# Products of softmax weights with values, taken for two key tiles together at every other step of the first attention

## The chip, the cores and the metric

The kernel runs on one core of a Trainium2 chip. The metric is the device time of one execution in microseconds (us). Before the change the median of three runs is 1603.94 us (1602.0 to 1604.71).

## The reference, cut to what matters

The whole program is a small transformer block for 1024 tokens of width 512: a first attention, a mixture-of-experts layer, a second attention with 4-bit weights, and the same mixture-of-experts layer again, each on a layer norm of the running sum `x`. The change touches only the first attention:

```python
q = hidden_state @ wq + bq          # 32 heads of 16
k = hidden_state @ wk + bk          # 8 groups of 16, each shared by 4 heads
v = hidden_state @ wv + bv
scores = jnp.einsum('bhqd,bhkd->bhqk', q, k) * scale
probs = jax.nn.softmax(scores, axis=-1)
out = jnp.einsum('bhqk,bhkd->bhqd', probs, v)
out = jnp.swapaxes(out, -1, -2).reshape(B, -1, HEAD_DIM * NUM_HEADS)
return out @ wo + bo
```

## The kernel before, in words

**Tiles.** The first attention goes through 16 pairs of heads (`PAIRS`), and for each pair through 8 tiles of 128 keys (`NT`). One (pair, key tile) is called a step here, so there are 128 steps, and a step is written (pair, kt).

**What a step computes.** Scores are computed twice. First with queries on the partitions, only to find each query's largest score: `half_score` (L333) is one matmul of 64 rows (L340) into a PSUM bank `sc` and one VectorE maximum over its 512 columns (L349). There are 512 of these, 4 in each step, and they run 40 ahead of the rest (`LEAD`), so that those of one pair are done during step 5 of the pair before it. When a pair's 32 are done, three small VectorE instructions (L352 to L354) join the halves and split the result into two parts in `largest`; `place_largest` (L359) turns that on TensorE (L363), copies it on ScalarE (L365) and lets SyncE's queue carry it to the rows of `ms_q` (L367).

Then the scores are computed again with keys on the partitions: `exponentials` (L376) takes for each of four parts `u` (two heads, two halves of the queries) one matmul (L381), one more that adds the negated maxima (L389), and the exponential on ScalarE (L393) into `pT`. `weighted` (L407) multiplies `pT` with the values: four matmuls (L414), whose outputs of 32 partitions lie side by side in one bank `po` and which run at once in four strips of 32 columns of the array. The trace holds two records for each, so a `weighted` shows as 8 records. After the last key tile, `po` is copied to `oT` (L423), which `tail` (L428) turns back (L434) and divides by the sums (L438, L439).

**Buffers.** There are 8 PSUM banks: three for `sc`, four for `st` (which `mp`, `pt`, `py` and `pp` share), one for `po`. `pT` has three buffers.

**Order.** On TensorE the order is the one written (L495, `manual_schedule`). On the other engines the tile framework lays the order down when the kernel is built, and it executes as laid down. `side_by_side` (L399) interleaves two chains: one on rows 0 to 63 of the array (three scores, the two matmuls of part 2, the fourth score), one on rows 64 to 127 (the two matmuls of parts 0, 1 and 3). A step therefore begins with six rounds, each of two matmuls that run at once in the two halves of the rows. The fourth score is in round six, and the rounds below are numbered so. After the rounds comes, at even key tiles, `place_largest` where maxima are ready, and then `weighted` of the step before (`behind`, L519). At `kt == 3` the tail of the pair before follows, at `kt` 5 and 7 of pairs 4, 8 and 12 a part of the output projection (`project_out`, L448), at `kt` 1 and 3 of pairs 3 and 7 the queries of later heads (`queries`, L287), and at `kt == 7` the loads of keys and queries for three pairs later (L298).

The scores are used up at step (14,5): 40 + 4 x 118 = 512. The last ten steps have none.

Of the kernel before, what the change touches and what calls it, by code (L numbers as in the profile page):

```python
# [41 lines left out]
def kernel(  # L42
# [159 lines left out]
    def attention_a():  # L202
# [6 lines left out]
        with ExitStack() as ph:  # L209
# [77 lines left out]
            def queries(c, half, *between):  # L287
                if half == 0:
                    q_hls[c] = work.tile([P, 2, S], F32R, tag="q_hl", name="q_hl")
                split(q_hls[c], ts(half, C), lambda k: wq_n[:, c, k], bq_sb[:, c : c + 1], *between)  # L290

            def stack_keys(g, eng):
                for r in range(8):
                    eng.dma_start(
                        ks[g % NS][ts(r, DA)].bitcast(F32), k_hl[ts(g, DA), r % 4 // 2].bitcast(F32)
                    )
# [16 lines left out]
            def values(t):  # L313
                pv = st_ps.tile([P, C], F32, tag="st", name="pv")
                for c in range(NC_):
                    nc.tensor.matmul(
                        pv[:, : G * DA],
                        xT[:, c, ts(t, P)],
                        wv_n[:, c, :],
                        start=(c == 0),  # L320
                        stop=(c == NC_ - 1),
                    )
                nc.vector.tensor_tensor(
                    v_sb[:, t, :, :DA],
                    pv[:, : G * DA].rearrange("p (g d) -> p g d", d=DA),
                    bv_b.rearrange("p (g d) -> p g d", d=DA),
                    ALU.add,
                )
# [30 lines left out]
            def place_largest():  # L359
                for pair in list(large):  # L360
                    both = large.pop(pair)
                    mp = st_ps.tile([P, C], F32, tag="st", name="mp")
                    nc.tensor.transpose(mp[:, :P], both.bitcast(F32), ident)  # L363
                    mT = work.tile([32, P], F32R, tag="mT", name="mT")
                    nc.scalar.copy(mT, mp[:32, :P])  # L365
                    for r in (0, 64):
                        nc.sync.dma_start(  # L367
                            ms_q[pair % 2][r : r + 2]
                            .bitcast(F32)
                            .rearrange("h j (t q) -> h (j t) q", q=P),  # L370
                            mT.bitcast(F32),
                        )
# [3 lines left out]
            def exponentials(pair, kt, u, rows):  # L376

                if u == 0:
                    pTs[pair, kt] = work.tile([P, 4, C], F32, tag="pT", name="pT", bufs=3)
                st = st_ps.tile([P, C], F32, tag="st", name="st")  # L380
                nc.tensor.matmul(  # L381
                    st,
                    ks[pair // 2 % NS][rows, ts(kt, P)],
                    qs[pair % NS][rows, u // 2, ts(u % 2, C)],
                    start=True,
                    stop=False,
                )
                yield
                nc.tensor.matmul(  # L389
                    st, ones[rows], ms_q[pair % 2][rows, u // 2, ts(u % 2, C)], start=False, stop=True  # L390
                )
                yield
                nc.scalar.activation(pTs[pair, kt][:, u], st, AF.Exp, scale=DA**-0.5)  # L393

            def chain(*parts):
                for part in parts:
                    yield from part

            def side_by_side(*two):  # L399

                two = list(two)
                while two:
                    for one in list(two):
                        if next(one, two) is two:
                            two.remove(one)

            def weighted(pair, kt):  # L407


                if kt == 0:  # L410
                    pos[pair] = av_ps.tile([P, C], F32, tag="po", name="po")
                po, pT = pos[pair], pTs.pop((pair, kt))
                for u in range(4):
                    nc.tensor.matmul(  # L414
                        po[ts(u, 32), :],
                        v_sb[:, kt, pair // 2, :],
                        pT[:, u],
                        start=(kt == 0),
                        stop=(kt == NT - 1),
                    )  # L420
                if kt == NT - 1:
                    oT = work.tile([P, C], F32, tag="oT", name="oT", bufs=1)
                    nc.vector.tensor_copy(oT, pos.pop(pair))  # L423
                    tails.append((pair, oT))
# [23 lines left out]
            def project_out(a, h):  # L448

                py = st_ps.tile([P, C], F32, tag="st", name="py")
                for c in range(NC_):
                    nc.tensor.matmul(  # L454
                        py,
                        o_sbs[a][:, 4 * h + c, :],
                        wo_n[:, c, :],
                        start=(c == 0),
                        stop=(c == NC_ - 1),
                    )  # L460
                nc.vector.tensor_tensor(x_sb[:, a, h, :], x_sb[:, a, h, :], py, ALU.add)
# [16 lines left out]

            LEAD = 40
            n_score = 0
            low, high = slice(0, 64), slice(64, 128)

            def next_score(rows):
                nonlocal n_score
                n_score += 1
                if n_score <= 32 * PAIRS:
                    yield from half_score(n_score - 1, rows)

            def scores(n):
                for _ in range(n // 2):
                    side_by_side(next_score(low), next_score(high))

            with tc.manual_schedule(engines={mybir.EngineType.PE}):  # L495
                for t in range(NT):
                    values(t)
                scores(4)
                for half in range(2):
                    queries(1, half, lambda: scores(2))  # L500
                scores(16)
                place_largest()
                scores(LEAD - n_score)
                behind = None
                for pair in range(PAIRS):
                    for kt in range(NT):
                        side_by_side(
                            chain(
                                next_score(low),
                                next_score(low),  # L510
                                next_score(low),
                                exponentials(pair, kt, 2, low),
                                next_score(low),
                            ),
                            chain(*[exponentials(pair, kt, u, high) for u in (0, 1, 3)]),
                        )
                        if kt % 2 == 0:
                            place_largest()
                        if behind is not None:  # L519
                            weighted(*behind)  # L520
                        behind = pair, kt
                        if kt == 3:
                            for item in tails:
                                tail(*item)
                            tails.clear()
                        if kt in (5, 7) and pair % 4 == 0 and pair:
                            project_out(pair // 4 - 1, (kt - 5) // 2)
                        if kt == 7 and pair + NS < PAIRS:
                            if (pair + NS) % 2 == 0:
                                stack_keys((pair + NS) // 2, nc.sync)  # L530
                            stack_queries(pair + NS)
                        if kt in (1, 3) and pair in (3, 7):
                            queries(pair // 4 + 2, kt // 2)
                weighted(*behind)

                for a in range(3):
                    norm.stats(a)
                norm.scale(0, 3)
                for item in tails:
                    tail(*item)  # L540
                for a in range(3):
                    xn = wq_in[:, 2 * (a % 2) : 2 * (a % 2) + 2]
                    norm.rows(a, xn)
                    norm.turned(
                        a, xn, lambda: st_ps.tile([P, C], F32, tag="st", name="tp"), False, to_xT
                    )
                    if a:
                        project_out(3, a - 1)
# [610 lines left out]
```

## Time and profile before

| | us |
|---|---|
| median of three runs | 1603.94 |
| the profiled execution, its own time | 1603.51 |
| its span, from first to last instruction | 1601.4 |
| steps with scores, 82 to 466 us of the span | 384 |
| steps without scores, 466 to 492 us | 26 |
| all after the first attention's steps, 492 us to the end | 1109 |

Busy time of the engines in these three stretches:

| stretch | TensorE | VectorE | ScalarE | granted clock |
|---|---|---|---|---|
| 82 to 466 us | 377.24 | 324.41 | 250.89 | 1.00 |
| 466 to 492 us | 25.97 | 1.60 | 19.53 | 1.00 |
| 492 to 1601 us | 1069.27 | 867.53 | 497.33 | 0.99 |

In the profile PE is TensorE's matmuls, PEld its weight loads, DVE is VectorE, ACT ScalarE, and SPq the queue of DMA issues on SyncE. A row of the timeline gives start, duration, engine, line, operation, output and inputs, and after x the number of instructions merged in it; behind it, in brackets, stands how long the engine was idle before and what released it. The duration of a merged row runs from the start of its first to the end of its last instruction. A busy TensorE is not TensorE at its peak, since matmuls are pipelined and their records overlap.

### The profile page before, as it was taken

The numbers are of one execution on the slowest core, as the hardware profiler recorded it, in microseconds if no ns is written. First come the engines' busy times: TensorE is split into PE (matmuls) and PEld (weight loads), VectorE is DVE, ScalarE is ACT, GpSimd is POOL, SyncE is SP. The second block draws the span as 40 slices with busy tenths as digits, with TensorE's granted clock in tenths as the row PEclk, the third lists the DMA queues.
The fourth block names the chain that finished last, engine by engine and source line by source line (L and its number), as shares of the span: only waits on it lengthen the run. The fifth ranks groups of instructions, "written<-read, shape, count | busy, mean of one in ns | idle before, by whom it ended". The sixth has DMA issues, their size and how long they took to land.

```text
span 1601.4 us, 24101 instructions
## 1 busy us (share of the span) xinstructions
PE 1535.4 (96%) x8119; PEld 994.2 (62%) x8119; DVE 1239.7 (77%) x2290; ACT 784.3 (49%) x1696; POOL 480.8 (30%) x380
## 2 busy tenths in 40 slices
PE   6899999999999989999999999999999999999978
PEld 3444444444445457777777777777777777777764
DVE  3798787799754586788888878888788788788763
ACT  2076565567674235544444544444444444454420
POOL 7000000000103144435436336336336335333120
PEclk9799999999999989999999999999999999999999
DMA  7523223223103233343343334333333333333311
GB/s 237 99 44 66 39 47 54 50 50 58 22 3 91 72 114 115 111 140 122 112 144 127 118 127 130 119 121 124 122 124 117 115 116 125 109 111 124 138 53 53
DMA packets 98010, 158.63 MB, mean 99 GB/s; under 512 B 14320, under 2 KB 53936, under 8 KB 97504
## 3 DMA queue, kind: packets, MB, share of 16 engines
q1 hardware_dynamic: 97024, 155.46, 32.5%
q0 software_dynamic: 864, 1.64, 0.7%
q8 instruction: 65, 1.06, 0.3%
q14 instruction: 57, 0.47, 0.1%
HBM read 33.03 MB, written 6.05 MB: 24 GB/s over the span
## 4 chain that ended last, share of the span: by engine, by line
PE 80%; DVE 11%; ACT 4%; issue 2%; DMA 1%; SPq 1%; POOL 1%; ACTq 0%; DVEq 0%; POOLq 0%
PE pc L877 16%; PE sc L835 14%; PE sc L340 6%; PE po L414 6%; PE pp L771 5%; DVE m L349 5%; PE pp L772 5%; PE tp L867 5%; PE py L771 4%; PE py L772 3%; PE bank L580 3%; PE pp L275 3%; PE st L381 2%; PE py L454 2%; PE st L389 1%
## 5 line engine op out<-in xcount | busy, mean ns | idle before, releaser
L349 DVE TENSOR_REDUCE m<-sc 128x1 f32<-128x512 f32 x512 | 320.0, 681 | 39.4 <-PE st L381 31.0
L844 ACT ACTIVATE x_sb<-sc,m 128x768 f32<-128x768 f32 (+7 forms) x256 | 189.9, 742 | 315.6 <-DVE m L840 310.0
L393 ACT ACTIVATE pT<-st 128x512 f32<-128x512 f32 x512 | 264.9, 603 | 126.6 <-PE st L389 102.5
L835 PE MATMUL sc<-kT,qT 128*128 128x512 f32 (+3 forms) x768 | 292.0, 489 | 3.8 <-ACT x_sb L844 2.4
L840 DVE TENSOR_REDUCE m<-sc 128x1 f32<-128x768 f32 (+7 forms) x256 | 192.6, 752 | 131.0 <-PE sc L838 129.7
L877 PE MATMUL pc<-xT,v_sb 128*128 128x256 f32 (+1 forms) x1024 | 247.8, 373 | 5.2 <-DVE acc L785 2.5
L340 PE MATMUL sc<-ks,qs 64*128 64x512 f32 x512 | 192.6, 464 | 9.8 <-DVE m L349 4.5
L846 DVE TENSOR_SCALAR x_sb<-x_sb,total 128x768 f32<-128x768 f32 (+7 forms) x256 | 189.0, 739 | 4.4
L877 PEld LDWEIGHTS pc<-xT,v_sb 128*128 128x128 f32 x1024 | 175.4, 189 | 22.0 <-DVE acc L785 3.2
L835 PEld LDWEIGHTS sc<-kT,qT 128*128 128x128 f32 x768 | 139.0, 192 | 74.8 <-issue 64.1
L340 PEld LDWEIGHTS sc<-ks,qs 64*128 64x128 f32 x512 | 86.7, 189 | 153.6 <-DVE m L349 130.6
L381 PE MATMUL st<-qs,ks 64*128 64x512 f32 x512 | 178.2, 426 | 1.6 <-ACT pT L393 0.2
L912 DVE SCALAR_TENSOR_TENSOR shared<-py,o_sc,shared 128x512 f32<-128x512 f32 x248 | 176.1, 739 | 4.0 <-PE py L772 3.9
L389 PE MATMUL st<-ms_q,ones 64*128 64x512 f32 x512 | 179.1, 414 | 0.0
L797 POOL TENSOR_TENSOR qT<-acc,cos_sb 128x512 f32<-128x512 f32 x62 | 81.9, 1320 | 301.3 <-DVE total L845 205.3
L771 PE MATMUL pp<-x_hl,w 128*128 128x512 f32 x384 | 167.0, 435 | 1.9 <-DVE acc L785 1.3
L868 ACT COPY xT<-tp 128x512 f32<-128x512 f32 (+2 forms) x320 | 137.4, 471 | 63.2 <-PE tp L867 62.9
L772 PE MATMUL pp<-x_hl,w 128*128 128x512 f32 x384 | 152.9, 398 | 2.3 <-DVE x_hl L729 2.3
L679 POOL TENSOR_SCALAR w<-r 128x512 fp32r<-128x512 int32 x80 | 122.6, 1532 | 105.5 <-PE pp L772 71.2
L785 DVE SCALAR_TENSOR_TENSOR acc<-pp,q_sc,acc 128x512 f32<-128x512 f32 x192 | 142.9, 745 | 13.5 <-ACT acc L783 5.8
L867 PEld LDWEIGHTS tp<-ident_r,moved 128*128 128x128 f32 x1152 | 125.3, 140 | 35.7 <-issue 2.0
L561 POOL TENSOR_TENSOR x_sb<-x_sb,shared 128x1024 f32<-128x1024 f32 x4 | 9.4, 2366 | 449.7 <-ACT wq_in L175 391.5
(167 smaller groups left out, 2303.3 us busy)
## 6 DMA issues: line engine op xcount, KB each, us to landing
turned<-acc SPq DMA_DIRECT2D x160, 128.0 KB
qs<-q_hl SPq DMA_DIRECT2D x256, 64.0 KB
moved<-x_sb SPq DMA_DIRECT2D x32, 512.0 KB
moved<-x_sb SPq DMA_DIRECT2D x32, 448.0 KB
moved<-x_sb SPq DMA_DIRECT2D x32, 384.0 KB
moved<-x_sb SPq DMA_DIRECT2D x32, 320.0 KB
r<-in_qwq_dram SPq DMA_DIRECT2D x32, 256.0 KB
r<-in_qwo_dram SPq DMA_DIRECT2D x32, 256.0 KB
```

The lines of the kernel that those rows point to most:

```text
L340: nc.tensor.matmul(sc, qs[pair % NS][rows, jj, ts(t, P)], ks[pair // 2 % NS][rows, ts(half, C)], start=True, stop=True,)
L349: nc.vector.tensor_reduce(ms[pair][:, at : at + 1], sc, AX.X, ALU.max, negate=True)
L381: nc.tensor.matmul(st, ks[pair // 2 % NS][rows, ts(kt, P)], qs[pair % NS][rows, u // 2, ts(u % 2, C)], start=True, stop=False,)
L389: nc.tensor.matmul(st, ones[rows], ms_q[pair % 2][rows, u // 2, ts(u % 2, C)], start=False, stop=True)
L393: nc.scalar.activation(pTs[pair, kt][:, u], st, AF.Exp, scale=DA**-0.5)
L771: nc.tensor.matmul(ps, lhsT, high, start=True, stop=False)
L772: nc.tensor.matmul(ps, lhsT, low, start=False, stop=True)
L835: nc.tensor.matmul(sc[:, k0:k1], qT[:, ts(t, P)], kT[:, k0:k1], start=True, stop=(k1 < keys))
L840: nc.vector.tensor_reduce(m, sc[:, :keys], AX.X, ALU.max, negate=True)
L844: nc.scalar.activation(p[:, :keys], sc[:, :keys], AF.Exp, bias=m, accum_out=total)
L867: nc.tensor.transpose(tp[:, k - k0, :].bitcast(F32R), p[:, ts(k, P)], ident_r)
L877: nc.tensor.matmul(pc[:, 2 * P * i + lo : 2 * P * (i + 1)], v_sb[:, k, ts(g, DB)], place[pair][:, k, lo:], start=(k == 0), stop=(k == 2 * ...
```

## The change

`behind` becomes a list. At an even key tile every step in it is taken through `weighted`, and the list is emptied; at an odd key tile nothing is multiplied with the values. So after an even step there come the products of two key tiles, 16 records in a row where there were 8. In step (p,0) these are tiles 6 and 7 of the pair before; in steps (p,2), (p,4), (p,6) they are tiles 0 and 1, 2 and 3, 4 and 5. The last two come after the loop.

```diff
-                behind = None
+                behind = []
                 for pair in range(PAIRS):
                     for kt in range(NT):
...
                         if kt % 2 == 0:
                             place_largest()
-                        if behind is not None:
-                            weighted(*behind)
-                        behind = pair, kt
+                        if kt % 2 == 0:
+                            for item in behind:
+                                weighted(*item)
+                            behind.clear()
+                        behind.append((pair, kt))
...
-                weighted(*behind)
+                for item in behind:
+                    weighted(*item)
```

In the built program, the numbers of instructions are the same on every engine. On VectorE the order changes as well: before, L352 to L354 stand after the fourth maximum of step (p,5), one behind the other. After, for all pairs but 4, 8, 12 and 14, they stand after the first, second and third maximum of step (p,6), one behind each. In pairs 5, 9 and 13 some statistics of the layer norm move by a few places. On ScalarE one row of the layer norm and four exponentials trade places, on SyncE's queue four of the loads of keys and queries do. Beyond the first attention no engine's order changes.

## Prediction

> **What bounds the kernel now.** I first read the 40 slices and the groups of the page: in the stage that changes, TensorE is busy everywhere and VectorE nearly so, so that neither share tells which of them sets the pace. I then asked for the waits between 82 and 493 us.
>
> ```profile
> engine line waited for: us in total, times, longest us
> ...
> PEld sc L340 <- DVE m L349: 115.7, 199, 1.2
> ...
> DVE m L349 <- PE st L381: 31.0, 72, 3.9
> ```
>
> The score's weight load waits for a maximum, because there are three `sc` banks. The maximum in turn waits for TensorE in most steps. They take turns, so the timeline of a step decides. Two plain steps on TensorE, and the same stretch on VectorE:
>
> ```profile
> 284.26 1.06 PE L414 MATMUL po<-pT,v_sb 128*32 128x512 f32 x8
> 285.25 0.49 PE L340 MATMUL sc<-ks,qs 64*128 64x512 f32 x1
> ...
> 285.59 0.39 PE L340 MATMUL sc<-ks,qs 64*128 64x512 f32 x1
> ...
> 285.82 0.39 PE L340 MATMUL sc<-ks,qs 64*128 64x512 f32 x1
> ...
> 286.53 0.50 PE L340 MATMUL sc<-ks,qs 64*128 64x512 f32 x1
> ...
> 286.97 1.06 PE L414 MATMUL po<-pT,v_sb 128*32 128x512 f32 x8
> ```
>
> ```profile
> 285.79 2.48 DVE L349 TENSOR_REDUCE m<-sc 128x1 f32<-128x512 f32 x4 [0.48 <-PE st L381]
> 288.50 2.48 DVE L349 TENSOR_REDUCE m<-sc 128x1 f32<-128x512 f32 x4 [0.22 <-PE st L381]
> 290.90 0.68 DVE L423 COPY oT<-po 128x512 f32<-128x512 f32 x1
> ```
>
> A plain step takes 286.97 - 284.26 = 2.71 us: 0.99 from the burst of L414 to the first round, then 1.72 of rounds. Four maxima take 2.48, each 0.68 long and (2.48 - 0.68) / 3 = 0.60 apart, so 4 x 0.60 = 2.40 of steady work. VectorE is idle only 0.22 a step: it lives through the burst on maxima in stock. The fourth score starts at 286.53, just as the first maximum is done (285.79 + 0.69 = 286.48). Both engines are at their limit.
>
> **The change part by part.** No instruction goes or comes. There are half as many bursts, each twice as long, and twelve rounds in a row.
>
> *The burst.* The second half of the records of L414 starts 0.45 after the first, and fp32 matmuls in a row (records of L275 at 263.12, 263.55, 263.98) start 0.43 apart. A double burst is thus 0.99 + 2 x 0.43 = 1.86, and at most 1.98.
>
> *A plain pair of steps, worked out.* Time 0 is the first round after a burst. From the rows above: rounds at 0, 0.33, 0.57, then each 0.23; the first maximum starts at 0.54, then one each 0.60; a bank is free 0.05 after its maximum; after a round that waited, the next comes 0.33 later; the burst follows an unwaited last round by 0.32 (301.50 to 301.83).
> - Maxima start at 0.54, 1.14, 1.74, 2.34, 2.94, 3.54, 4.14, 4.74; each ends 0.68 later, the first at 1.23, the last at 5.42.
> - Scores 1 to 3 at 0, 0.33, 0.57; 4 (round 6) at 1.28; 5 needs the second maximum's bank: 1.87; 6 the third's: 2.47; 7 the fourth's: 3.07; 8 (round 12) at 3.07 + 0.33 + 0.23 + 0.23 = 3.86, its bank being free at 3.67.
> - Burst from 3.86 + 0.32 = 4.18 to 6.04.
>
> So 6.04 in place of 2 x 2.71 = 5.42: **+0.62**. At the burst's start VectorE has 5.42 - 4.18 = 1.24 of work in stock, and the next maximum comes 1.86 + 0.54 = 2.40 later: it idles 1.16 where it idled 2 x 0.22.
>
> *The price of the array's change of form, weighed.* Around a burst the trace shows 0.54 from its second half to the next round (0.43 within a row), 0.33 to the second round (0.23), 0.32 at the entry (0.23): 0.30 for each burst. The Trainium skill, TensorEngine Tiling (Array Packing), Key Properties, says that changing the tiling mode, not just the tile, drains the array. By this rule alone, one change fewer in each of the 59 pairs of steps with scores (to step (14,5)) would give 59 x 0.30 = 18 us of gain. By the rows the gain lies within TensorE's time, which the working above already has, while the maxima set the end. The rule's saving is real, but goes into waiting.
>
> *The four kinds of pairs of steps.* Before, from the starts of L414:
> - Steps 1 and 2, 2.98 + 2.71 = 5.69. The copy of `po` stands before the next maximum. Now VectorE is idle when the burst ends, so it costs only 0.20 (maximum at 0.74 in place of 0.54): 6.24, +0.55.
> - Steps 3 and 4, 3.75 (298.08 to 301.83) + 2.71 = 6.46. The tail now lies between the rows. Its transposes run from 1.71 to 2.29, the fifth score goes at 2.29, later ones at 2.63, 3.07. The tail's four small VectorE steps (0.6 to 0.8 together, between maxima) delay maxima 5 to 8 to 3.06, 3.98, 4.73, 5.33. One `st` bank is held by the tail, so part 3 waits for the exponential of part 0, to 3.80 (as at 301.17 before), and the burst goes at 4.46: 6.32, -0.14.
> - Steps 5 and 6, 2.71 + 3.28 = 5.99. L352 to L354 now stand after maxima 5, 6 and 7. VectorE takes its queue in order, so L354 comes behind three more maxima: 2.94 + 0.60 (L352 at 3.54), maximum at 3.66, L353 at 4.27, maximum at 4.39, L354 at 5.0 to 5.18. The transpose L363 stands on TensorE before the burst and waits for that: 5.24 where the rounds would let it go at 4.3. Then 0.26 to the burst as before, and 1.86: 7.36, **+1.37**. Behind L363 queue the burst and every later score.
> - Steps 7 and 0: plain, 6.04, +0.62.
>
> *Count.* Plain kinds: 9 of the first at 0.55 and pair 0 (three steps before the first burst) at 0.5; 11 of the second at -0.14, pair 0 without a tail at +0.62; 11 of the third at 1.37, pair 14 at +0.25; 11 of the fourth at 0.62. That is 5.5 - 0.9 + 15.3 + 6.8 = 26.7. In ten pairs of steps a block of 3.6 us (`queries`, `project_out`) lies between the rows; VectorE catches up in it, and one entry and exit is saved: 10 x -0.17 = -1.7. In pairs 5, 9, 13 layer-norm steps of VectorE fall into its new idle time: -1.2. Without scores, ScalarE's exponentials (0.48 apart, 8 in a pair of steps, four `st` banks) hold the rows by 0.2 in four pairs of steps: +0.8. Sum **+24.6 us**, before to after, in one profiled execution of 1603.51 us (its span of 1601.4 and 2.1 around it); that execution lies 0.4 us under the median, so I put the median at 1603.94 + 24.6 = 1628.5.
>
> *What I cost at nothing.* `pT`: with three buffers an exponential of an odd step needs the buffer that the first half of the burst reads; the next exponential starts some 0.86 after the rows begin, and both halves are over by then. Without that cover it would be 0.43 a pair of steps. `po`: its next use now comes two steps after the copy. `ms_q`: L363 to first use was 4.3 us (252.93 to 257.23) and is 4.6. The moved loads on SyncE's queue have a pair of heads (24 us) to land, and the transfer share is 0.26 here; nothing waits for them before beyond 0.3 us. After the loop the chain on TensorE goes on as before, so 492 us and later are only shifted.
>
> *Bounds.* No row shows maxima with a double burst. Best for VectorE: all three banks full at the burst's start, 1.80 in stock: it still idles 0.60, and a plain pair takes 4.88 + 0.60 = 5.48, no gain. So the plain kinds can't go below zero by more than the trace's grain; with the mixed pairs at -3 and the second kind at -1.5 the lower bound is about -5 us. Upper: if the tail and the norm steps hide nothing, 12 x 0.76 + 1.2 = 10 us more. The wait at L363 is the largest single unknown: 0 to 0.94 us, 11 times. I take its full value, as VectorE's order is laid down and its pace of 0.60 is the nearest row.
>
> **The rivals.**
> 1. *TensorE sets the end, and the saved changes of form are gained.* Price -0.30 a burst, 59 times: 1604 - 18 = 1586, faster. For it: TensorE is the busiest engine, with 80% of the chain. It decides from the point where VectorE's stock at the burst reaches 2.40 us, four maxima; three banks hold 1.80. Against it stands the 0.22 of idle after each single burst.
> 2. *L363 doesn't wait*, because L354 comes earlier than worked out: 11 x 0.75 less, 1628.5 - 8 = 1620. For it: before, L363 never waited for L354 (only 3.8 us for ScalarE, 15 times). Against it: the order of the built program.
> 3. *The tail hides nothing*: steps 3 and 4 lose as plain ones do, 11 x 0.76 more, 1637.
> 4. *No change*: the starved maxima are made good by the mixed pairs and the emptier chain, 1604.
>
> **How the numbers follow.** My working 0.66, rival 2 0.18, rival 3 0.09, rival 4 0.03, rival 1 0.04. The predicted time is the first's, 1628.5. The range reaches over rival 2, with 4 us for its own errors, and to rival 3: 1616 to 1637. About 0.2% is what a measurement of this kernel can tell from no change. Faster 0.04, same 0.03, slower 0.93.
>
> **What would show it.** In the changed profile a plain pair of steps takes about 6.0 us between bursts; the burst of L414 shows 16 records in 1.9 us; VectorE's idle time before L349 grows from 32.6 us in this stage to 70 or more (59 x 0.72 more at the most), with L381 or L340 as releaser; L363 waits for L354 by 0.9 in pairs without a projection; in steps 3 and 4 the period is about 6.3. The stage from 82 to 492 us is longer by 24, the rest is not. I am wrong if the plain pair stays at 5.4 or less (rival 1 or 4), if L354 ends before the twelfth round (rival 2), or if the stages after the first attention move.

## The result, and the profile after

The changed kernel takes 1626.16 us, the median of four runs (1625.74 to 1627.03), where the kernel before, measured alongside, takes 1602.97 (1598.57 to 1604.71). The ratio is 1.0149 (95% interval 1.0131 to 1.0166). The medians differ by 23.2 us and the ratio makes it 24, where 24.6 was worked out. The profiled execution has a span of 1623.6 us, 22.2 more than before.

The same plain pair of steps that the prediction worked out, here steps (5,7) and (6,0) on TensorE and then on VectorE:

```profile
235.88 1.93 PE L414 MATMUL po<-pT,v_sb 128*32 128x512 f32 x16
237.73 0.50 PE L340 MATMUL sc<-ks,qs 64*128 64x512 f32 x1
...
238.07 0.39 PE L340 MATMUL sc<-ks,qs 64*128 64x512 f32 x1
...
238.30 0.39 PE L340 MATMUL sc<-ks,qs 64*128 64x512 f32 x1
...
239.01 0.49 PE L340 MATMUL sc<-ks,qs 64*128 64x512 f32 x1
...
239.61 0.50 PE L340 MATMUL sc<-ks,qs 64*128 64x512 f32 x1
...
240.21 0.50 PE L340 MATMUL sc<-ks,qs 64*128 64x512 f32 x1
...
240.80 0.50 PE L340 MATMUL sc<-ks,qs 64*128 64x512 f32 x1
...
241.61 0.39 PE L340 MATMUL sc<-ks,qs 64*128 64x512 f32 x1
...
241.93 0.64 PE L414 MATMUL po<-pT,v_sb 128*32 128x512 f32 x4
```

```profile
238.26 4.88 DVE L349 TENSOR_REDUCE m<-sc 128x1 f32<-128x512 f32 x8 [2.17 <-PE sc L340]
243.92 0.69 DVE L423 COPY oT<-po 128x512 f32<-128x512 f32 x1 [0.78 <-PE po L414]
```

The burst is one row of 16 records, 1.85 us to the next round. The first three scores come at once; then scores 4 to 7 come 0.60 apart, the pace of the maxima, because each waits for its bank, as the weight load of the fifth shows:

```profile
239.61 0.18 PEld L340 LDWEIGHTS sc<-ks,qs 64*128 64x128 f32 x1 [0.41 <-DVE m L349]
```

The eight maxima run without a gap for 4.88 us, end at 243.14, and the next score is not there before the burst from 241.93 is over: VectorE stands idle. From burst to burst 241.93 - 235.88 = 6.05 us, 5.42 before.

The pair of steps with L352 to L354, (5,5) and (5,6), on VectorE and at its end on TensorE:

```profile
230.97 3.08 DVE L349 TENSOR_REDUCE m<-sc 128x1 f32<-128x512 f32 x5 [0.90 <-PE st L381]
233.97 0.16 DVE L352 TENSOR_TENSOR m<-m 128x16 f32<-128x16 f32 x1
234.06 0.68 DVE L349 TENSOR_REDUCE m<-sc 128x1 f32<-128x512 f32 x1
234.66 0.16 DVE L353 CAST largest<-m 128x16 fp32r<-128x16 f32 x1
234.73 0.68 DVE L349 TENSOR_REDUCE m<-sc 128x1 f32<-128x512 f32 x1
235.33 0.17 DVE L354 TENSOR_TENSOR largest<-m,largest 128x16 fp32r<-128x16 f32 x1
235.41 0.68 DVE L349 TENSOR_REDUCE m<-sc 128x1 f32<-128x512 f32 x1
```

```profile
235.64 0.30 PE L363 MATMUL mp<-ident,largest 128*128 128x128 f32 x1 [0.94 <-DVE largest L354]
```

L354 stands behind three maxima and ends at 235.50; L363 has waited 0.94 us for it, and the burst behind L363 with it. In the kernel before, the same three stood together at the start of that stretch, and L363 had no wait:

```profile
227.68 0.18 DVE L352 TENSOR_TENSOR m<-m 128x16 f32<-128x16 f32 x1
227.89 0.17 DVE L353 CAST largest<-m 128x16 fp32r<-128x16 f32 x1
228.10 0.17 DVE L354 TENSOR_TENSOR largest<-m,largest 128x16 fp32r<-128x16 f32 x1
```

```profile
229.36 0.33 PE L363 MATMUL mp<-ident,largest 128*128 128x128 f32 x1
```

The periods of pairs of steps, from the starts of the bursts in the two traces (in "mixed" pairs of steps queries or a part of the projection lie between the rows, in "plain" ones not):

| steps | plain, before | plain, after | worked out | mixed, after less before |
|---|---|---|---|---|
| 1 and 2 | 5.70 | 6.26 | 6.24 | -0.22 |
| 3 and 4 | 6.45 | 6.32 | 6.32 | -0.13 |
| 5 and 6 | 5.99 | 7.28 | 7.36 | -0.14 |
| 7 and 0 | 5.41 | 6.05 | 6.04 | -0.16 |

All 62 pairs of steps between the bursts of steps (0,2) and (15,6) take 402.7 us before and 426.7 after, 24.0 more. With the ends of the loop, from the first L381 to the start of the last burst, it is 24.5 more (413.2 and 437.7). The span grew by less, 22.2: the loop started 3.5 us earlier in the execution after (first L381 at 73.5 us, before at 77.0), where the two programs are the same, and from the last burst on the two need 1111.1 and 1112.4 us. The prediction put both at nothing. The early start fits the granted clock, whose mean up to the first L381 is 0.89 after (8.1 us short of full clock) and 0.85 before (11.6 us short), but no run tested it.

The wait list of the changed stage, 82 to 516 us:

```profile
PEld sc L340 <- DVE m L349: 102.1, 220, 0.8
...
DVE m L349 <- PE st L381: 41.2, 36, 2.9
...
DVE m L349 <- PE sc L340: 25.0, 12, 2.2
...
PE mp L363 <- DVE largest L354: 10.3, 11, 0.9
```

From the list of the kernel before, besides the two lines that the prediction shows:

```profile
DVE m L349 <- PE sc L340: 1.4, 4, 0.5
```

Before its maxima VectorE waits in fewer places (36 and 12, before 72 and 4) and for longer: 66.2 us in all, before 32.4. The last line of the changed kernel's list is new: eleven waits, 0.9 each.

### The profile page after: what moved, and what is told of

Its sections match the earlier page's. It is cut to its first block, busy times and chain, and to the rows that moved or that the text cites. A ratio compares the mean times of both kernels' runs of the same rounds, so it can differ in the third digit from the quotient of the medians.

```text
span 1623.6 us, 24111 instructions
## 1 busy us (share of the span) xinstructions
PE 1543.5 (95%) x8119; PEld 1002.9 (62%) x8119; DVE 1234.1 (76%) x2290; ACT 789.6 (49%) x1696; POOL 480.2 (30%) x380
## 3 DMA queue, kind: packets, MB, share of 16 engines
HBM read 33.03 MB, written 6.05 MB: 24 GB/s over the span
## 4 chain that ended last, share of the span: by engine, by line
PE 55%; DVE 4%; ACT 2%; issue 1%; DMA 0%; POOL 0%; ACTq 0%; DVEq 0%; SPq 0%
PE pc L881 16%; PE sc L839 15%; PE pp L775 5%; PE pp L776 5%; PE tp L871 4%; PE py L775 3%; PE py L776 3%; PE bank L584 1%; DVE m L844 1%; PE sc L842 1%; PE bank L572 1%; DVE acc L789 1%; ACT x_sb L848 1%; ACT xT L872 0%; PE bank L645 0%
## 5 line engine op out<-in xcount | busy, mean ns | idle before, releaser
L349 DVE TENSOR_REDUCE m<-sc 128x1 f32<-128x512 f32 x512 | 318.6, 680 | 71.7 <-PE st L381 41.2
L393 ACT ACTIVATE pT<-st 128x512 f32<-128x512 f32 x512 | 268.9, 604 | 148.1 <-PE st L389 138.6
L340 PE MATMUL sc<-ks,qs 64*128 64x512 f32 x512 | 208.2, 469 | 15.3 <-DMA qs<-q_hl 2.9
L839 PEld LDWEIGHTS sc<-kT,qT 128*128 128x128 f32 x768 | 139.5, 192 | 74.7 <-issue 63.9
L381 PE MATMUL st<-qs,ks 64*128 64x512 f32 x512 | 184.9, 435 | 0.6 <-ACT pT L393 0.2
```

What stands on the lines that cost most here:

```text
L340: nc.tensor.matmul(sc, qs[pair % NS][rows, jj, ts(t, P)], ks[pair // 2 % NS][rows, ts(half, C)], start=True, stop=True,)
L349: nc.vector.tensor_reduce(ms[pair][:, at : at + 1], sc, AX.X, ALU.max, negate=True)
L381: nc.tensor.matmul(st, ks[pair // 2 % NS][rows, ts(kt, P)], qs[pair % NS][rows, u // 2, ts(u % 2, C)], start=True, stop=False,)
L839: nc.tensor.matmul(sc[:, k0:k1], qT[:, ts(t, P)], kT[:, k0:k1], start=True, stop=(k1 < keys))
```

## The experiments

Theory S is the prediction's: the three score banks hold too little work for VectorE to live through a double burst. Rival T: the long burst or the twelve rounds are slow on TensorE itself. Rival A: the exponentials on ScalarE set the pair of steps. All periods below are those of plain pairs of heads, from the starts of the bursts of L414 (L417 where lines are added ahead of it).

**VectorE and ScalarE taken out of the way.** Two kernels, from the one before and the changed one:

```diff
-                nc.vector.tensor_reduce(ms[pair][:, at : at + 1], sc, AX.X, ALU.max, negate=True)
+                nc.vector.tensor_reduce(ms[pair][:, at : at + 1], sc[:, : C // 4], AX.X, ALU.max, negate=True)
...
-                    pTs[pair, kt] = work.tile([P, 4, C], F32, tag="pT", name="pT", bufs=3)
+                    pTs[pair, kt] = pT_all[(NT * pair + kt) % 3]
...
-                nc.scalar.activation(pTs[pair, kt][:, u], st, AF.Exp, scale=DA**-0.5)
+                nc.scalar.activation(pTs[pair, kt][:, u, : C // 4], st[:, : C // 4], AF.Exp, scale=DA**-0.5)
```

`pT_all` (its lines are left out) are three tiles that are made once and filled with 1.0 ahead of the loop.

Expected of the first:

> The kernel before, with each maximum taken over the first 128 of its 512 columns and each exponential over the first 128 of its 512 queries (the rest of the weights stay at 1.0): VectorE and ScalarE should no longer hold anything, so TensorE alone sets a step. All theories: a plain step 2.57 us (0.99 + 0.33 + 4 x 0.23 + 0.32), where the kernel before has 2.71. It is the base for the next run.

Expected of the second:

> The changed kernel with the same two cuts. Theory S (VectorE starves in the double burst, because three score banks hold too little): with VectorE out of the way only the saved change of the array's form is left: 0.33 + 10 x 0.233 + 0.32 + 1.86 = 4.84 for a plain pair of steps against 5.14, so -0.30, and some 19 us less than the base over 64 pairs of steps. Rival T (the double burst or the twelve rounds in a row are slow on TensorE itself): a pair stays at 5.4 or more, and the kernel is no faster than the base.

Measured: 1574.01 us (1572.12 to 1579.79) with single bursts and 1563.63 (1561.02 to 1565.89) with double ones. Against the kernel before the ratios are 0.9825 (0.9796 to 0.9854) and 0.9759 (0.9733 to 0.9786), so the double bursts now **gain** some 10 us, half of the 19 that I expected. A plain pair takes 5.16 and 5.02, and in the steps without scores 5.15 to 5.19 and 4.83. So rival T falls: TensorE itself is faster with double bursts. The saving of 0.30 a pair, which the prediction read from the rows, shows whole (0.32 to 0.36) only where there are no scores. With scores it is 0.14, because one wait for a bank is left. The sixth and seventh score of a plain pair with double bursts:

```profile
212.31 0.39 PE L340 MATMUL sc<-ks,qs 64*128 64x512 f32 x1
...
212.62 0.18 PEld L340 LDWEIGHTS sc<-ks,qs 64*128 64x128 f32 x1 [0.33 <-DVE m L349]
212.62 0.50 PE L340 MATMUL sc<-ks,qs 64*128 64x512 f32 x1
```

The seventh score starts 0.31 after the sixth, not 0.23, and takes 0.50; its weight load, which waited for a maximum, starts with it and not ahead of it. The round after it comes 0.34 later. It needs the bank of the fourth score, three rounds before: even a maximum of 0.29 us is not done in three rounds of 0.23.

**Only the maxima shortened** (the first hunk alone):

> The kernel before with only the maxima cut to 128 of 512 columns. Theory S: VectorE idle, ScalarE keeps up with single bursts: a plain step 2.58 to 2.60, as in the ten steps without scores.

> The changed kernel with only the maxima cut. Theory S: the starved maxima were the bound, and next is ScalarE through its four banks, as in the steps without scores (5.46 a pair there): a plain pair 5.2 to 5.5, so 0.55 to 0.85 less than 6.05. Rival A (ScalarE's exponentials were the bound all along, the maxima only wait with them): a plain pair stays at 6.0.

Measured, one execution each: 1584.57 and 1591.40 us. Steps 7 and 0 took 5.53 to 5.66 with single bursts, above what I expected (5.16 to 5.20, which steps 1 and 2 did take), and 5.49 with double ones, as expected. With single bursts the first use of `ms_q` in step (p,0) now waits for its transfer, 0.36 in the mean, about what is missing:

```profile
PEld st L389 <- DMA ms_q<-mT: 4.3, 12, 0.4
```

Rival A falls, since 6.05 became 5.49 by VectorE alone. But with short maxima the double bursts gain nothing either. They cost about 0.3 in steps 1 and 2 and in steps 5 and 6: now 108 weight loads of L381 wait for an exponential's bank (28 with single bursts, 16.8 us).

```profile
PEld st L381 <- ACT pT L393: 31.8, 108, 1.6
```

So there are two stocks, three banks for VectorE and four for ScalarE, and the longer burst outlasts both.

**The number of score banks**, two, three and four, in the changed kernel. For two only `sc` is changed, from 3 to 2. For four, `st` must give one up, so ScalarE is taken out of the way by the exponential's cut above, and a base with three is run the same way:

```diff
-            sc_ps = pool(ph, "a_sc_ps", 3, PSUM)
-            st_ps = pool(ph, "a_st_ps", 4, PSUM)
+            sc_ps = pool(ph, "a_sc_ps", 4, PSUM)
+            st_ps = pool(ph, "a_st_ps", 3, PSUM)
```

> The changed kernel with two score banks in place of three. Theory S: VectorE has one maximum less in stock when the burst begins, so a plain pair of steps grows by about 0.6, to 6.65 to 6.75 us (worked out: score 8 at 4.43, burst from 4.86 to 6.72). Rivals T and A: the number of score banks doesn't matter, 6.05.

> The changed kernel with three score banks and three st banks, each exponential over the first 128 of its 512 queries (the rest of the weights stay at 1.0), so that ScalarE holds nothing. Base for the next run. Theory S: unchanged, a plain pair of steps 6.05 us, because the maxima set it. Rival A (the exponentials set it): well under 6, towards 5.2.

> The same with four score banks and three st banks. Theory S: one maximum more in stock, 0.60 less idle: a plain pair of steps 5.44 to 5.5. Rivals T and A: as the run with three score banks.

| score banks | whole kernel, one execution | steps 7 and 0 | expected | VectorE idle before the copy of `po` that follows |
|---|---|---|---|---|
| two | 1687.28 | 6.83 | 6.65 to 6.75 | 1.19 |
| three (exponentials cut) | 1640.43 | 6.05 | 6.05 | 0.79 |
| four (exponentials cut) | 1637.47 | 5.46 | 5.44 to 5.5 | 0.19 |

Burst to burst with four banks:

```profile
240.00 1.92 PE L417 MATMUL po<-pT,v_sb 128*32 128x512 f32 x16
...
243.12 0.66 PE L340 MATMUL sc<-ks,qs 64*128 64x512 f32 x2
...
245.12 0.40 PE L340 MATMUL sc<-ks,qs 64*128 64x512 f32 x1
...
245.45 1.49 PE L417 MATMUL po<-pT,v_sb 128*32 128x512 f32 x11
```

A fourth and fifth score now stand one behind the other with no wait between. The fourth bank is one maximum, 0.60 us, in stock, and moves the pair by 0.59. With the exponentials cut and three banks the pair stays at 6.05, which speaks against rival A once more. With two banks the pair is 0.78 longer than in the changed kernel: VectorE also has gaps within the rows (its eight maxima take 5.24 in place of 4.88), which I had not counted. Both kernels with three `st` banks lose elsewhere: steps 3 and 4 take 7.07, where the tail holds one of them, so their whole times don't show what a bank is worth. With four score banks steps 5 and 6 stay at 7.28 in most pairs of heads: there L354 decides, not the bank. In three of them (pairs 2, 7 and 11) steps 5 and 6 take 7.28 to 7.41 and steps 7 and 0 take 6.95 to 7.15 in place of 5.46. Their double burst takes 3.42 to 3.61 us in place of 1.92, because the granted clock stood at half:

```profile
148.63 3.42 PE L417 MATMUL po<-pT,v_sb 128*32 128x512 f32 x16
```

```profile
core 0: us, PE busy (x) PEld busy (x) DVE busy (x) ACT busy (x) POOL busy (x), PEclk, DMA share, GB/s
...
149.00:150.00 1.00, 1.00 (x8) 0.20 (x4) 0.00 (x0) 0.00 (x0) 0.00 (x0) 0.50 0.00 0
```

L363 has waited 1.5 us for L354 just before, but it does so in eleven pairs of heads (1.36 to 1.53), and why the clock fell in three of them stays open. In the kernel before and in the changed one the granted clock is 1.00 from 82 us to the last burst, so it has no part in the 24 us.

**The wait at L363.**

```diff
-            LEAD = 40
+            LEAD = 44
...
-                        if kt % 2 == 0:
+                        if kt == 6:
                             place_largest()
```

> The changed kernel with the scores 44 ahead in place of 40, and the maxima placed only at kt 6: a pair's last score falls a step earlier, so L354 should long be done when L363 comes up. Theory S with the wait at L363 as worked out: steps 5 and 6 go from 7.28 to between 6.3 and 6.65 us, and the kernel loses 7 to 11 us against the changed one (some 1617). Rival: the 0.9 us of wait only moves to another place (ScalarE, the load of ms_q or VectorE's queue): under 3 us less.

Measured: 1619.01 us, median of four (1615.69 to 1622.91); ratio to before 1.0115 (1.0078 to 1.0152), span of the profiled execution, the fastest of the four, 1613.6. Steps 5 and 6 take 6.32, the others what they took. The sum of the pairs of steps falls from 426.7 to 415.8, by 10.9. VectorE has L352 to L354 behind it before the first maximum of the pair:

```profile
227.91 0.17 DVE L352 TENSOR_TENSOR m<-m 128x16 f32<-128x16 f32 x1
228.12 0.17 DVE L353 CAST largest<-m 128x16 fp32r<-128x16 f32 x1
228.32 0.17 DVE L354 TENSOR_TENSOR largest<-m,largest 128x16 fp32r<-128x16 f32 x1
228.79 4.87 DVE L349 TENSOR_REDUCE m<-sc 128x1 f32<-128x512 f32 x8 [0.29 <-PE sc L340]
```

So by the steps of the traces nearly half of the change's 24 us is this wait, which the change brought about only through VectorE's order, and it doesn't move elsewhere. The whole kernels are a weaker witness: their medians differ by 7.2 us, at the low end of what was expected, and the two intervals of the ratio just overlap (the changed kernel's begins at 1.0131).

**A version that beats both.** The kernel before with single bursts, relieved where the study showed VectorE short; and the same with double bursts only where other work lies between the rows. The first:

```diff
-            LEAD = 40
+            LEAD = 44
...
-                        if kt % 2 == 0:
+                        if kt == 6:
                             place_largest()
...
-                    nc.vector.tensor_copy(both[:, 0:16], m[:, 0:16])
-                    nc.vector.tensor_tensor(
+                    nc.gpsimd.tensor_copy(both[:, 0:16], m[:, 0:16])
+                    nc.gpsimd.tensor_tensor(
                         both[:, 16:32], m[:, 0:16], both[:, 0:16].bitcast(F32), ALU.subtract
...
-                    nc.vector.tensor_copy(oT, pos.pop(pair))
+                    nc.scalar.copy(oT, pos.pop(pair))
```

The second has these edits in the changed kernel, and instead of its `if kt % 2 == 0:` ahead of `weighted`:

```diff
-                        if kt % 2 == 0:
+                        held = (
+                            kt == 3
+                            or (kt == 1 and pair in (3, 7))
+                            or (kt in (5, 7) and pair in (4, 8, 12))
+                        )
+                        if not held:
                             for item in behind:
                                 weighted(*item)
                             behind.clear()
                         behind.append((pair, kt))
```

> The kernel before, with single bursts, the scores 44 ahead and the maxima placed at kt 6 alone, L353 and L354 on GpSimd, and the copy of po on ScalarE: VectorE is relieved of 0.35 + 0.6 us for each pair of heads, and L363 waits for nothing. Theory S: steps 5 and 6 from 5.99 to about 5.7 (TensorE's 0.26 for L363 stays), steps 1 and 2 from 5.70 to about 5.45, the others unchanged: 0.55 a pair of heads, 13 times, so 7 us less than before, some 1596. Rival: the copy on ScalarE delays the exponentials by as much as VectorE gains: no change.

> The same, and the products of two key tiles together only where other TensorE work lies between the rows anyway: steps 3 and 4 (the tail), and the pairs of steps with queries or an output projection. From the changed kernel's own trace: 12 x 0.13 + 2 x 0.22 + 6 x 0.15 = 2.9 us less than the run above, some 1593. Rival (two products together cost wherever they are): as the run above or slower.

Measured: 1599.35 us for the first (1593.04 to 1605.09; ratio 0.9972, 0.9960 to 0.9984), 1594.00 for the second (1590.93 to 1599.27; ratio 0.9946, 0.9928 to 0.9964), 1603.89 for the kernel before. By the medians the first gains 4.5 us and the second 9.9. The sums of the pairs of steps are 402.7 before, 396.4 and 392.9. By these the first gains 6.3 where 7 was expected (steps 1 and 2 at 5.42, steps 5 and 6 at 5.75), the second another 3.5 where 2.9 was. The intervals of the two ratios overlap a little, so that the second is better than the first rests on the steps of the traces more than on the medians.

## Why the prediction was right, point by point

- *The sum, +24.6.* Measured from the first L381 to the last burst: +24.5. What lies outside the loop was put at nothing; it was -3.5 ahead of it and +1.2 behind it in the profiled execution. The median, 1626.16, lies 2.3 under the predicted 1628.5; about one of these 2.3 is that the kernel before itself came out at 1602.97 and not at 1603.94.
- *Both engines at their limit, VectorE living on its stock through a burst.* Shown: from two to three to four banks the pair of steps goes from 6.83 to 6.05 to 5.46, about one maximum each.
- *The double burst, 1.86.* Measured 1.85 to the next round.
- *The plain pair, 6.04.* Measured 6.05. Scores 5, 6 and 7 were worked out at 1.87, 2.47 and 3.07 after the first; they came at 1.88, 2.48 and 3.07.
- *One change of the array's form fewer, 18 us by itself, which would go into waiting.* Shown: with VectorE and ScalarE out of the way the double bursts do gain, 0.34 a pair without scores; in the changed kernel nothing of it is left in plain pairs. This agrees with the rule that the prediction took from the Trainium skill, TensorEngine Tiling (Array Packing), Key Properties, but that the saved time is a drain of the array no run shows.
- *Steps 1 and 2, 3 and 4.* 6.26 and 6.32, worked out 6.24 and 6.32. Rival 3 falls with the second: the tail does hide the wait.
- *Steps 5 and 6, +1.37, with the wait at L363 the largest unknown.* Measured +1.30, with a wait of 0.94. A small step delays the maximum behind it by 0.07 to 0.09 us (233.97 to 234.06, 234.66 to 234.73), where I had set 0.12. Rival 2 was wrong, as the order in the built program had said.
- *Mixed pairs, -0.17.* Measured -0.13 to -0.22.
- *VectorE's idle time before L349, 70 us or more.* Missed: measured 66.1. The rest stands before the copy of `po`, which I had left out of that line: 0.78 in each of the eleven pairs of heads whose steps 7 and 0 are plain and have scores, 8.6 in all, where it was nothing before; together 74.7.
- *Pairs 5, 9, 13: -1.2.* Measured -0.08, -0.09 and, in pair 13, +0.50 and -1.25: -0.9. *Steps without scores, +0.8:* measured -0.02, +0.28, -0.11 and +0.57 for the four pairs of steps from (14,7) to (15,6), +0.7 in all; the sum was right, the even share of 0.2 was not.
- *What was put at nothing* in the loop stayed at nothing: no wait for `pT`, and 0.2 us in all for `ms_q`.

Rival 1 failed at the point that it named: the stock would have had to reach 2.40 us. In the row above of three banks the maxima end 1.21 after the burst's start (243.14 and 241.93); with four banks it was 1.81 (247.26 and 245.45), and the pair took 5.46, no less than with single bursts.

## What to carry to other kernels

When TensorE feeds another engine through PSUM banks and then turns to other work, that engine lives on what stands in the banks: compare banks x time of one consumer instruction with the length of the other work plus the time to the first new result. That product is the most that the stock can be (1.80 here, of which 1.21 were there when the burst began), so it has to be clearly more than that sum. Making such blocks longer saves changes of the array's form (0.30 us each here), and costs the whole of what the stock doesn't cover; it pays where the consumer has a pause of other origin anyway. After a change in the order of one engine, read the new order of the others too: by the traces, a small instruction that slipped behind three large ones was 11 of 24 us. And after each limit look for the next: with short maxima it was the exponentials' banks, and in steps 7 and 0 the transfer of `ms_q`.

## What was not expected of the hardware

A bank costs more than the time of the instruction that empties it. With maxima of 0.29 us and three banks TensorE still waited once a pair of steps: 0.39 of matmul (from 211.85), 0.04 to the maximum's start (212.28), 0.29 and 0.05 are 0.77, more than three rounds of 0.23. The score that had to wait for a bank also shows 0.50 in place of 0.39, and the round after it came 0.34 later in place of 0.23. Its weight load started with it (both at 212.62), that of the score before 0.23 ahead of it (212.08 and 212.31); that the one is the cause of the other was not tested.
